# Two graph layers over 32 batches: h of batch 30 and three y tiles of batch 31 in the ring of x, and a new table of planned times

## The chip, the cores and the metric

The kernel runs on one core of a Trainium2 chip. The metric is the time of one launch on the device, in microseconds (us). The engines of the core each run their own queue in order: PE (matrix products), DVE (vector), ACT (scalar functions), POOL (GpSimd), SP (here only an issuer of DMAs). An engine waits at an instruction until what it needs is there, and everything queued behind it waits too.

## The reference

Input x is [32, 512, 1024] (batch, channel c, node n) in f32, adj is [512, 512].

```
h = max(layernorm(x, last axis), 0)
q = sum_c wq[c] h[b,c,n] ;  k = sum_c wk[c] h[b,c,n]
scores[b,m,n] = leaky_relu(k[b,m] + q[b,n], 0.01)
att = softmax(scores over n)
agg[b,c,m] = sum_n h[b,c,n] att[b,m,n]
y = x + relu(adj @ agg + bm)
h = max(layernorm(y), 0)
out = y + einsum('bnf,nm->bmf', h, adj * adj) + bias
```

The last line contracts the channel axis with the elementwise square of adj; bm is added to the last product as well in the kernel's finish step, since turn leaves it out (it adds max(agg, -bm), which is relu(agg + bm) - bm).

## The kernel before

**Layer 0 without the score matrix.** Because a score depends only on the sum of two numbers and leaky relu has two slopes, the softmax of a row splits the nodes, sorted by q, in two sets at one place. So the kernel sorts the nodes by q, forms weighted running sums over the sorted values, and each output node picks two rows out of the running sums. The nodes are 8 blocks of 128, the channels NC = 4 tiles of 128; a sorted table has NB = 9 blocks.

For each batch b these steps run, in this order of data (the name is that of a Python function; the tile that the trace shows stands in brackets):

- load (four x tiles, DMAs on SP, L306), stats0 (DVE, L319), norm0 and slopes0, relu0 in place (ACT, L337);
- scores (PE, pq, then ACT sends it to DRAM), row (ACT's DMA queue reads it back on all partitions, qrow), columns (PE transposes it, pr, to qk);
- rank (DVE, 8 steps, counts how many q are smaller) and to_rows (two halves of 4, gives the scatter rows idx); lower (ACT, 8 steps, counts for the output side) and from_rows (DVE, gives the gather rows idg); factors (DVE and ACT);
- value (PE, pv, 8 steps of 4 products, L454), spread (ACT, PSUM to v, L461), scatter (POOL, 8 indirect DMAs, L467) into a table td in DRAM; there are TABLES = 5 tables;
- fetch (SP, 6 DMAs, L484) reads the sorted table back as vs; weights (ACT, w, L493 and L496), later (DVE, wc and e), totals (PE, pd, L516 and L517, and den on DVE), stationary (POOL, sm, L527, three times for three blocks each);
- scan (PE, sc, 9 steps per batch, L540 and L543), each followed by sums (ACT, L552 to L556: one row each of two vs tiles takes the carry, so that the next scan depends on it; then t, which SP stores to the table);
- gather (POOL, 8 indirect DMAs, L564) into g, of which there is one buffer; excess, divide (DVE), weigh (ACT, L589), combine (DVE, 16 steps, L593);
- reload (four y tiles: x again from HBM, SP, L311), turn (PE transposes g, tr, L600; DVE adds it to y, L602).

Layer 1 is stats1, norm1, slopes1, relu1 (ACT writes h, L337), lift (DVE adds the bias to y, L343), propagate (PE, pg, 8 steps of 4 products, L607), finish (DVE, L615, with the store to out on SP).

**Rings.** x tiles have 7 buffers (pool xp, and 7 more of yp in the first batches), y tiles 7 (yp), h tiles NC = 4 (hp), v 8, vs 5 (three per batch), t 2, g 1. PSUM has 8 banks in one ring. A new tile takes the buffer that was released first and waits for its last reader.

**The order.** Nothing is scheduled automatically. Every step of every batch gets a planned time, b*T + PLAN[name][n] with T = 80.4 (L621), in the first five and last five batches moved by a shift and a stretch from FIRST and LAST (plan, L623). The steps are sorted by this time (L668) and emitted in that order under manual_schedule; each engine's queue is thus a cut of one list. The times serve only to sort. Where batches overlap, PE's list holds value steps of batch b+1, scans of b and b-1, propagate steps of batch b-3 and turns of b-2.

Of the kernel before, what the change touches and what calls it, by code (L numbers as in the profile page):

```python
# [16 lines left out]
P = 128  # L17
# [10 lines left out]
    "adjacency": (-107.86,),  # L28
    "biases": (73.25,),
    "columns": (2.54,),  # L30
    "combine": (
        293.1, 294, 295.37, 296.17, 294.24, 294.54, 295.16, 296.42, 294.48,
        294.66, 293.61, 295.28, 294.87, 296.68, 296.01, 296.52,
    ),
    "compare_mask": (-77.25,),
    "divide": (278.91,),
    "excess": (272.83,),
    "factors": (28.83,),
    "fetch": (74.87,),
    "finish": (357.8, 362.86, 376.29, 376.42, 388.63, 415.81, 401.13, 417.85),  # L40
    "from_rows": (89.36,),
    "gather": (250.12, 258.6, 255.35, 261.49, 268.91, 253.59, 258.29, 256.1),
    "later": (82.34,),
    "lift": (341.79, 343.89, 354.9, 347.45),
    "load": (-125.04, -82.54, -104.22, -58.22),
    "lower": (26.37, 18.82, 14.83, 28.33, 13.66, 12.67, 46.5, 36.18),
    "masks": (-12.78,),
    "norm0": (-27.69,),
    "norm1": (323.91,),
    "pads": (1.15,),  # L50
    "propagate": (347.57, 348.71, 350.13, 365.41, 372.81, 382.23, 382.61, 392.3),
    "rank": (16.85, 14.2, 18.53, 15.82, 17.42, 21.57, 23.3, 23.64),
    "reload": (275.48, 285.03, 274.13, 289.84),
    "relu0": (-17.18, -15.69, -15.67, -14.84),
    "relu1": (334.79, 335.4, 335.54, 338.3),
    "row": (1.98,),
    "scan": (89.28, 94.78, 102.87, 122.08, 139.17, 152.12, 172.91, 183.19, 200.42),
    "scatter": (39.55, 42.53, 43.86, 40.7, 49.58, 45.37, 44.59, 45.6),
    "scores": (-1.83,),
    "slopes0": (-22.22,),  # L60
    "slopes1": (324.32,),
    "spread": (10.78, 16.46, 5.24, 10.37, 28.25, 25.74, 19.08, 20.35),
    "square": (53.38,),
    "stationary": (83.36, 116.24, 162.19),
    "stats0": (-63.29, -60.88, -63.05, -41.14),
    "stats1": (318.79, 319.93, 319.41, 319.38),
    "sums": (89.92, 97.06, 115.14, 127.32, 141.99, 156.22, 174.86, 189.46, 207.26),
    "to_rows": (23, 29.08),
    "totals": (88.21,),
    "turn0": (303.69, 304.68, 304.05, 304.98),  # L70
    "turn1": (312.19, 312.02, 311.8, 312.15),
    "turn_adjacency": (-39.9,),
    "value": (3.89, 14.52, -1.07, 4.1, 20.69, 18.74, 15.77, 15.86),
    "weigh": (286.66, 289.32, 286.94, 289.3, 287.24, 286.87, 287.56, 291.05),
    "weights": (79,),
}
FIRST = {
    "columns": ((-37.98, 0), (-10.89, 0), (-8.73, 0), (-1.59, 0), (-5.53, 0)),
    "combine": ((-1.47, -0.283), (2.11, 0.074), (6.02, -0.446), (-3.46, 1.643), (-3.02, -0.662)),
    "divide": ((0.43, 0), (-4.84, 0), (5.31, 0), (-0.36, 0), (-5, 0)),  # L80
    "excess": ((6.36, 0), (0.71, 0), (9.39, 0), (2.63, 0), (1.02, 0)),
    "factors": ((14.45, 0), (42.49, 0), (37.13, 0), (-13.47, 0), (3.3, 0)),
    "fetch": ((-0.33, 0), (-9.12, 0), (-3.14, 0), (-6.37, 0), (-4.73, 0)),
    "finish": ((0.35, -0.506), (-4.34, -0.255), (-1.3, 0.166), (-13.48, -0.751), (-1, -0.145)),
    "from_rows": ((-17.73, 0), (122.52, 0), (-12.48, 0), (-3.68, 0), (39.28, 0)),
    "gather": ((-3.91, 0.337), (8.03, -0.392), (-0.23, 0.924), (1.48, -0.818), (-10.72, 0.312)),
    "later": ((-6.32, 0), (-2.49, 0), (-5.11, 0), (-3.44, 0), (5.07, 0)),
    "lift": ((5.78, 0.249), (-7.64, -0.77), (14.78, 1.406), (9.87, -0.096), (12.09, 1.113)),
    "load": ((-114.53, -0.719), (-41.9, -0.581), (-61.5, -0.134), (-67.36, 0.974), (-10.03, 0.381)),
    "lower": ((-4.18, -0.847), (-10.86, -0.761), (3.36, -0.598), (31.38, 0.125), (27.64, -0.444)),  # L90
    "norm0": ((-48.85, 0), (-42.24, 0), (-15.97, 0), (-23.37, 0), (-5.52, 0)),
    "norm1": ((-4.55, 0), (0.86, 0), (5.16, 0), (-3.3, 0), (2.66, 0)),
    "propagate": ((3.18, -0.698), (0.66, -0.203), (-2.02, -0.096), (-5.59, -0.325), (1.62, -0.11)),
    "rank": ((-4.4, 0.497), (1.55, -0.098), (-9.21, 1.126), (4.42, 0.365), (7.2, -0.023)),
    "reload": ((2.37, 0.404), (2.84, 0.512), (6.15, -0.047), (4.83, 0.053), (5.08, 0.729)),
    "relu0": ((-52.67, -0.811), (-32.9, 0.887), (-5.05, 1.412), (-5.92, -0.277), (0.27, -0.952)),
    "relu1": ((4.34, 0.844), (-4.2, 0.375), (9.88, -0.496), (1.58, 0.346), (-1.74, -0.782)),
    "row": ((-2.93, 0), (-19.24, 0), (-8.82, 0), (3.92, 0), (-1.39, 0)),
    "scan": ((-8.07, -0.009), (-4.12, 0.027), (-4.42, -0.075), (-2.52, 0.062), (-0.12, -0.002)),
    "scatter": ((19.59, 0.356), (0.39, -0.164), (-11.93, -0.276), (15.6, -0.115), (8.6, 0.613)),  # L100
    "scores": ((-48.13, 0), (-16.76, 0), (-5.07, 0), (-5.89, 0), (-6.97, 0)),
    "slopes0": ((-51.56, 0), (-32.21, 0), (-9.48, 0), (-3.65, 0), (3.28, 0)),
    "slopes1": ((3.12, 0), (1.34, 0), (13.39, 0), (3.58, 0), (5.29, 0)),
    "spread": ((3.65, -0.128), (-4.12, 0.811), (6.73, -0.135), (3.45, 0.185), (7.08, 1.002)),
    "stationary": ((-16.55, -0.278), (-1, 0.017), (-1.03, 0.007), (-4.23, -0.058), (4.88, -0.025)),
    "stats0": ((-86.5, 0.491), (-55.52, 0.533), (-26.5, 0.735), (-39.6, 0.274), (-0.81, 0.405)),
    "stats1": ((-2.32, 0.867), (-1.78, -0.548), (-2.88, 0.916), (-1.4, -0.748), (0.94, 0.179)),
    "sums": ((-4.03, -0.009), (-3.78, 0.04), (-3.01, -0.086), (-3.05, 0.043), (0.68, 0.024)),
    "to_rows": ((-6.46, 0.165), (-1.64, -0.568), (-5.7, -0.361), (5.62, -0.493), (8.82, -0.906)),
    "totals": ((-7.21, 0), (-4.95, 0), (-6.35, 0), (-3.7, 0), (-0, 0)),  # L110
    "turn0": ((1.54, 1.026), (5.01, 1.316), (7.07, -0.842), (11.23, 1.597), (7.25, 0.74)),
    "turn1": ((-5.63, 2.282), (4.23, 0.277), (-3.42, -0.878), (-9.56, -0.462), (0.94, 1.931)),
    "value": ((-14.35, 0.282), (-16.49, 0.638), (-1.63, 0.411), (-4.93, 0.45), (-4.23, 0.018)),
    "weigh": ((-1.72, 0.361), (-2.31, -0.775), (10.15, 0.018), (-5.33, 0.803), (-1.65, 0.186)),
    "weights": ((-3.94, 0), (-0.72, 0), (-2.63, 0), (-0.65, 0), (3.83, 0)),
}
LAST = {
    "columns": ((4.26, 0), (-3.03, 0), (2.37, 0), (-0.77, 0), (3.86, 0)),
    "combine": ((164.15, 0.268), (7.89, -0.595), (-1.54, 0.851), (5.2, 1.047), (1.56, -0.96)),
    "divide": ((162.11, 0), (3.32, 0), (-8.28, 0), (1.71, 0), (-3.58, 0)),  # L120
    "excess": ((127.64, 0), (-3.09, 0), (-3.12, 0), (2.67, 0), (0.92, 0)),
    "factors": ((-11.15, 0), (-18.33, 0), (1.07, 0), (-11.1, 0), (-11.56, 0)),
    "fetch": ((-1.81, 0), (-1.04, 0), (-0.37, 0), (-0.32, 0), (-3.1, 0)),
    "finish": ((699.4, -0.546), (150.27, -0.075), (20.88, 0.53), (4.22, 0.22), (6.11, 0.071)),
    "from_rows": ((13.84, 0), (-28.23, 0), (48.43, 0), (-17.87, 0), (17.41, 0)),
    "gather": ((88.35, 0.017), (-13.92, -0.31), (-9.45, 0.61), (-5.67, 0.718), (-2.02, 0.573)),
    "later": ((7.83, 0), (2.55, 0), (2.21, 0), (-1.95, 0), (-0.28, 0)),
    "lift": ((585.22, -0.837), (120.6, 0.105), (1.56, -0.183), (-6.91, -0.419), (9.05, -0.044)),
    "load": ((1.51, 0.156), (-2.49, 0.009), (4.84, -0.047), (9.16, -0.437), (7.85, -0.154)),
    "lower": ((9.16, 0.14), (-5.44, 0.016), (-5.91, -0.205), (-2.69, 0.118), (-12.14, -0.652)),  # L130
    "norm0": ((-2.04, 0), (-6.51, 0), (-2.65, 0), (-11.04, 0), (5.36, 0)),
    "norm1": ((418.29, 0), (27.36, 0), (-0.04, 0), (-2.45, 0), (1.02, 0)),
    "propagate": ((526.78, -0.74), (151.44, 0.764), (12.38, 0.445), (9.65, 0.206), (11.26, 0.117)),
    "rank": ((4.79, 0.609), (3.43, 0.076), (-8.9, -0.909), (-5.02, -0.932), (1.67, 0.09)),
    "reload": ((184.29, -0.585), (23.97, -0.873), (-3.56, 0.841), (1.54, 0.226), (-3.06, -0.231)),
# [27 lines left out]
def kernel(  # L163
# [169 lines left out]
    def relu(s, layer, c):  # L333
        h = s.x[c]
        if layer == 1:
            h = hp.tile([P, N], F32, tag="h", name=f"h_{s.b}_{c}")
# [362 lines left out]
```

## Time and profile before

| | |
|---|---|
| time before, median of 3 | 2385.05 us (2382.75 to 2387.69) |
| profiled execution | 2390.79 us, span 2389.1 us |
| mean granted clock of PE | 0.985 |
| PE busy | 2298.7 us, 96% of the span |
| DVE, ACT, POOL busy | 1957.4, 1589.4, 719.5 us |
| propagate, L607 | 2048 products, 908.4 us |
| value, L454 | 2048 products, 906.5 us |
| scan, L543 | 1024 products, 287.5 us |
| DMA | 643.45 MB, 269 GB/s over the span |

"Span" is the time between the first and last instruction in the profile. Busy time of PE counts the products; weight loads overlap them. A profile line such as "PE pd L516 <- ACT w L493: 10.2, 3, 4.8" reads: PE stood before line 516 (which writes pd) for ACT's w of line 493, in total 10.2 us, three times, at most 4.8 us. In a table by stretch each line has the window, its length, the busy time of PE, PE's weight loads, DVE, ACT and POOL with the count of their instructions, the granted clock of PE (1.00 is full), the busy share of the DMA engines and GB/s; a table for PE alone has only its busy time.

### The profile page before, as it was taken

The page shows a single profiled execution, that of the slowest core. Times are in us where ns is not written, and L with a number is a line of the kernel's source. Part 1 is how long each engine was busy: PE and PEld are TensorE (multiplying, and loading weights), DVE is VectorE, ACT ScalarE, POOL GpSimd, SP SyncE. Part 2 cuts the span into 40 slices and gives each one's busy share as a digit, 9 for nine tenths or more (in the row PEclk, how much of TensorE's full clock was granted, in tenths as well). Part 3 has the DMA queues.
Part 4 walks back from the last instruction along what each step waited for, and adds up shares of the span by engine and source line. Part 5 has one row for each costly group of instructions (what it writes and reads, how often), then busy time and mean ns, then how long its engine had stood idle before and what let it go on. Part 6 is the DMA issues. An engine that isn't in the chain of part 4 may idle for free.

```text
span 2389.1 us, 28172 instructions
## 1 busy us (share of the span) xinstructions
PE 2298.7 (96%) x7568; PEld 1016.2 (43%) x7568; DVE 1957.4 (82%) x5008; ACT 1589.4 (67%) x2878; POOL 719.5 (30%) x973
## 2 busy tenths in 40 slices
PE   7787999999999999999999999999999999999897
PEld 3233434444444444444444444444444444444343
DVE  6457978788988888988888898888898878889675
ACT  4576666766776766776676677676676856676450
POOL 2233323232332233233223233223323233223310
PEclk9898999999999999999999999999999999999898
DMA  7679887988988998988998888899998888988872
GB/s 231 154 188 279 275 286 256 302 256 269 300 284 284 289 293 258 290 294 268 293 305 261 272 291 285 285 289 282 273 281 277 281 279 250 290 267 282 290 294 87
DMA packets 206895, 643.45 MB, mean 269 GB/s; under 512 B 29120, under 2 KB 29248, under 8 KB 206736
## 3 DMA queue, kind: packets, MB, share of 16 engines
q1 hardware_dynamic: 142944, 355.74, 52.3%
q0 software_dynamic: 57344, 268.99, 30.9%
q10 hardware_dynamic: 6448, 16.92, 2.2%
q8 instruction: 61, 1.00, 0.2%
q14 instruction: 98, 0.80, 0.1%
HBM read 429.94 MB, written 211.60 MB: 269 GB/s over the span
## 4 chain that ended last, share of the span: by engine, by line
PE 84%; DMA 7%; DVE 4%; ACT 3%; issue 1%; SPq 1%; POOL 0%; ACTq 0%; DVEq 0%; POOLq 0%
PE pg L607 35%; PE pv L454 31%; PE sc L543 10%; PE tr L600 4%; DMA vs<-td 3%; PE pq L349 2%; DMA td<-t 2%; PE sc L540 1%; DVE g L593 1%; DVE st L319 1%; DMA qd<-qr 1%; DVE junk L396 1%; DMA wqk<-in_L_gnn_wk_dram 1%; DMA g<-td,idg 1%; SPq L484 0%
## 5 line engine op out<-in xcount | busy, mean ns | idle before, releaser
L607 PE MATMUL pg<-h,wsq 128*128 128x512 f32 x2048 | 908.4, 597 | 12.1 <-ACT h L337 11.9
L454 PE MATMUL pv<-wmT,x 128*128 128x512 f32 x2048 | 906.5, 597 | 1.1 <-ACT x L337 1.0
L607 PEld LDWEIGHTS pg<-h,wsq 128*128 128x128 f32 x2048 | 382.6, 190 | 513.3 <-issue 475.9
L454 PEld LDWEIGHTS pv<-wmT,x 128*128 128x128 f32 x2048 | 381.8, 191 | 495.8 <-issue 457.6
L527 POOL TENSOR_TENSOR sm<-mask_a,wc 128x192 f32<-128x192 f32 x96 | 57.3, 596 | 1128.5 <-DVE wc L504 718.8
L593 DVE SCALAR_TENSOR_TENSOR g<-g,cf 128x512 f32<-128x512 f32 x512 | 363.2, 777 | 6.4 <-ACT g L589 3.6
L467 POOL DMA_INDIRECT td<-v,idx x256 | 285.1, 1114 | 251.7 <-POOL v L466 41.4
L564 POOL DMA_INDIRECT g<-td,idg x256 | 244.0, 953 | 193.9 <-issue 67.9
L543 PE MATMUL sc<-vs,sm 128*64 128x512 f32 x1024 | 287.5, 629 | 12.5 <-ACT vs L552 4.9
L407 ACT ACTIVATE junk<-qrow,qk 128x1024 bf16<-128x1024 f32 x256 | 294.7, 1151 | 6.3 <-DVE qk L370 2.9
L552 ACT COPY vs<-sc 1x512 f32<-1x512 f32 x256 | 145.1, 567 | 214.4 <-PE sc L543 150.3
L602 DVE SCALAR_TENSOR_TENSOR y<-tr,nbm,y 128x512 f32<-128x512 f32 x256 | 176.0, 743 | 56.7 <-PE tr L600 52.0
L615 DVE SCALAR_TENSOR_TENSOR y<-pg,bm_sb,y 128x512 f32<-128x512 f32 x256 | 186.2, 734 | 34.4 <-PE pg L607 34.4
L555 ACT COPY t<-sc 128x512 f32<-128x512 f32 x288 | 168.3, 585 | 66.4 <-DMA td<-t 49.7
L396 DVE TENSOR_SCALAR_CACHE_REDUCE junk<-qrow,qk,cnt 128x896 bf16<-128x896 f32 (+6 forms) x224 | 180.4, 805 | 8.2
L337 ACT ACTIVATE x<-x,nmr,rstd 128x1024 f32<-128x1024 f32 x128 | 148.8, 1231 | 38.4 <-DVE nmr L330 38.4
L391 DVE TENSOR_SCALAR_CACHE_REDUCE junk<-qrow,qk 128x128 bf16<-128x128 f32 (+6 forms) x224 | 164.9, 736 | 8.2 <-issue 2.4
L461 ACT COPY v<-pv 128x512 f32<-128x512 f32 x256 | 140.6, 583 | 44.8 <-issue 28.3
L319 DVE BATCH_NORM_STATS2 st<-x 128x6 f32<-128x512 f32 x256 | 162.1, 675 | 7.1 <-DMA x<-in_x_dram 7.1
L589 ACT ACTIVATE g<-g,cf 128x512 f32<-128x512 f32 x256 | 163.4, 712 | 1.9 <-DVE cf L583 1.9
L343 DVE TENSOR_TENSOR y<-y,bias_sb 128x1024 f32<-128x1024 f32 x128 | 156.6, 1230 | 7.9 <-ACT h L337 7.9
L319 DVE BATCH_NORM_STATS2 st<-y 128x6 f32<-128x512 f32 x256 | 159.1, 663 | 0.0
(111 smaller groups left out, 1913.3 us busy)
## 6 DMA issues: line engine op xcount, KB each, us to landing
vs<-td SPq DMA_DIRECT2D x192, 384.8 KB
td<-t SPq DMA_DIRECT2D x576, 128.2 KB
x<-in_x_dram SPq DMA_DIRECT2D x128, 512.0 KB
y<-in_x_dram SPq DMA_DIRECT2D x128, 512.0 KB
out_dram<-y SPq DMA_DIRECT2D x128, 512.0 KB
qrow<-qd ACTq DMA_DIRECT2D x32, 512.0 KB
td<-v,idx POOLq DMA_INDIRECT x256, 8.3
g<-td,idg POOLq DMA_INDIRECT x256, 13.4
```

The lines of the kernel that those rows point to most:

```text
L319: nc.vector.bn_stats(st[:, i, :], s.x[c][:, ts(i, HALF)])
L396: nc.vector.tensor_scalar(junk[:, j * P :], s.qrow[:, j * P :], qc, first, ALU.is_lt, ALU.add, accum_out=s.cnt[:, 1, j : j + 1],)
L407: nc.scalar.activation(junk, s.qrow, AF.Sign, bias=s.qk[:, 1, j : j + 1], accum_out=s.sgn[:, j : j + 1])
L454: nc.tensor.matmul(pv, s.h[c][:, ts(j, P)], wmT[:, c, :], start=(c == 0), stop=(c == NC - 1))
L467: i = nc.gpsimd.indirect_dma_start(tds[s.b % TABLES][:, :], bass.IndirectOffsetOnAxis(ap=s.idx[j // 4][:, j % 4 : j % 4 + 1], axis=0), v[: ...
L543: nc.tensor.matmul(p[ts(k, HP), :], m[:, k, :], s.vs[h][:, 0:C], start=True, stop=True)
L555: nc.scalar.copy(t[:, 0:C], p)
L564: nc.gpsimd.indirect_dma_start(s.g[:, j, :], None, tds[s.b % TABLES][0 : 3 * NB * HP, :].rearrange("(s k) w -> s (k w)", k=3), bass.Indire ...
L593: nc.vector.scalar_tensor_tensor(r, s.g[:, j, k * W : k * W + C], s.cf[:, k, j : j + 1], r, ALU.mult, ALU.add)
L602: nc.vector.scalar_tensor_tensor(xh, pt, nbm[:, o : o + 1], xh, ALU.max, ALU.add)
L607: nc.tensor.matmul(pg, wsq[:, r, ts(c, P)], s.h[r][:, ts(i, HALF)], start=(r == 0), stop=(r == NC - 1),)
L615: nc.vector.scalar_tensor_tensor(xh, s.pg.pop((c, i)), bm_sb[:, c : c + 1], xh, ALU.add, ALU.add)
```

## The change

Four things, none of which adds or drops a product, a vector step or a DMA:

- h tiles of batch 30 (B - 2) are taken from the ring of x instead of that of h;
- y tiles 0, 1 and 2 of batch 31 are taken from the ring of x instead of that of y;
- load and reload have a planned time and shifts for each of the four tiles;
- all times in PLAN, FIRST and LAST, and T, are new.

The last one changes the order of the queues. On PE the steady batches keep their order except for a few exchanges: value step 3 before 0, propagate (3, 0) before (2, 1), one turn step later, scan 2 of batch b before scan 7 of batch b - 1. The first five and last five batches change more. On ACT the order needs two more loads of function tables (123 for 121), among the first and the last batches.

```diff
 PLAN = {
...
-    "load": (-125.04, -82.54, -104.22, -58.22),
+    "load0": (-132.547,),
+    "load1": (-83.561,),
+    "load2": (-110.642,),
+    "load3": (-58.45,),
...
-    "propagate": (347.57, 348.71, 350.13, 365.41, 372.81, 382.23, 382.61, 392.3),
+    "propagate": (346.423, 349.207, 352.169, 365.765, 371.233, 382.761, 381.981, 389.706),
-    "rank": (16.85, 14.2, 18.53, 15.82, 17.42, 21.57, 23.3, 23.64),
+    "rank": (17.984, 18.872, 20.129, 19.992, 25.594, 25.16, 26.367, 26.318),
...
-    "scan": (89.28, 94.78, 102.87, 122.08, 139.17, 152.12, 172.91, 183.19, 200.42),
+    "scan": (88.672, 94.082, 102.974, 119.344, 135.342, 151.67, 171.394, 183.726, 197.836),
...
-    "to_rows": (23, 29.08),
+    "to_rows": (21.507, 28.041),
...
-    "value": (3.89, 14.52, -1.07, 4.1, 20.69, 18.74, 15.77, 15.86),
+    "value": (4.654, 14.383, -2.141, 4.319, 19.868, 19.769, 15.801, 17.456),
...
     def reload(s, c):
-        t = yp.tile([P, N], F32, tag="y", name=f"y_{s.b}_{c}")
+        pool, tag = (xp, "x") if s.b == B - 1 and c < NC - 1 else (yp, "y")
+        t = pool.tile([P, N], F32, tag=tag, name=f"y_{s.b}_{c}")
...
         if layer == 1:
-            h = hp.tile([P, N], F32, tag="h", name=f"h_{s.b}_{c}")
+            pool, tag = (xp, "x") if s.b == B - 2 else (hp, "h")
+            h = pool.tile([P, N], F32, tag=tag, name=f"h_{s.b}_{c}")
...
-    T = 80.4
+    T = 80.647
...
         for f in (
-            load, reload, lift, rank, lower, value, spread, scatter, to_rows, scan, sums, gather,
-            weigh,
+            lift, rank, lower, value, spread, scatter, to_rows, scan, sums, gather, weigh,
         ):
...
+        for c in range(NC):
+            plan(s, load, f"load{c}", c, args=((),))
+            plan(s, reload, f"reload{c}", c, args=((),))
```

FIRST and LAST hold a pair (shift, stretch) for each of five batches and each name in the same way, all of them new.

## The prediction

> **What bounds the kernel now.** I read the page first, then a table of engine time by stretch of the span, then the waits of PE, then the chain that ended last.
>
> ```profile
> span 2389.1 us, 28172 instructions
> PE 2298.7 (96%) x7568; PEld 1016.2 (43%) x7568; DVE 1957.4 (82%) x5008; ACT 1589.4 (67%) x2878; POOL 719.5 (30%) x973
> ```
>
> PE is busy for 2298.7 of 2389.1 us, so a new order of the same work can win at most the 90 us in which it stands, plus what a slow clock costs. The table by stretch (PE's time first, then the other engines, the granted clock, DMA) says where those lie:
>
> ```profile
> 60.00:160.00 100.00, 82.25 (x245) 31.17 (x248) 51.17 (x176) 69.55 (x135) 24.60 (x44) 0.91 0.63 157
> 160.00:200.00 40.00, 36.12 (x110) 13.58 (x102) 26.57 (x92) 18.36 (x45) 11.92 (x16) 0.96 0.95 292
> 200.00:250.00 50.00, 36.89 (x144) 18.02 (x145) 38.84 (x99) 37.21 (x69) 18.99 (x25) 0.86 0.93 281
> ...
> 300.00:600.00 300.00, 293.26 (x974) 130.24 (x972) 245.15 (x638) 205.21 (x372) 91.78 (x123) 0.99 0.85 273
> 600.00:1200.00 600.00, 599.77 (x1980) 265.25 (x1977) 522.88 (x1349) 424.86 (x770) 194.85 (x261) 1.00 0.90 286
> ...
> 2200.00:2250.00 50.00, 40.03 (x128) 18.39 (x128) 31.38 (x68) 26.31 (x53) 11.53 (x14) 0.86 0.94 292
> ...
> 2340.00:2390.00 50.00, 33.65 (x93) 15.91 (x90) 22.07 (x35) 4.93 (x5) 0.00 (x0) 0.83 0.16 63
> ```
>
> From 600 to 1200 us PE is full, and the next 600 us are alike (600.00 of 600): no order gains there, it can only lose. PE stands for 34.7 us between 60 and 250 (the first batches fill the pipeline), 6.7 in 300 to 600, 10.0 in 2200 to 2250, 16.3 in the last 50; the first 14.3 are the load of wqk, which stays. What PE waits for, up to 300 us and then from 2150 on:
>
> ```profile
> PE sc L540 <- ACT vs L553: 11.7, 3, 7.7
> PE pd L516 <- ACT w L493: 10.2, 3, 4.8
> PE tr L600 <- DVE g L593: 4.4, 1, 4.4
> ...
> PE pg L607 <- ACT h L337: 11.9, 2, 10.7
> PE pd L516 <- ACT w L493: 7.5, 1, 7.5
> PE sc L543 <- ACT vs L552: 2.3, 1, 2.3
> ```
>
> "pd waits for w" is the arrival of a batch's fetch from the table, ACT's weights being a 0.5 us step behind it. The chain shows the loop of the fill: fetch lands, DVE ranks the next batch, indices, eight scatters on POOL, next fetch. The last fetch of the fill, and a hand-over of the tail (start, us, what):
>
> ```profile
> 222.04 10.77 DMA vs<-td
> ...
> 2292.69 7.14 DMA y<-in_x_dram
> 2299.83 2.63 DVE y L602 x4
> ```
>
> In the fill pd of batches 0 to 4 starts at 70.6, 119.5, 169.7, 235.2 and 308.6, each 0.4 to 2.4 us after its fetch has landed (70.2, 119.0, 169.3, 232.8, 308.2). So a stall between two of these gains nothing by going away, unless the next fetch lands earlier: PE would only wait longer at the next pd. The prices of what is moved: a propagate or value step is 3.5 us, a scan about 1.0, a turn step 0.44.
>
> **The change part by part.**
>
> *The two ring edits.* h of batch 30 no longer waits for the readers of h of batch 29, h of batch 31 no longer for those of batch 30; three y tiles of batch 31 no longer wait for an out transfer. In the trace h_31 is computed at 2352.44, when its slopes are just ready (2351.97), 12.9 us after batch 30's last propagate ended; h_30 at 2309.72 with slopes at 2309.63 and pg_29 ended at 2309.79. The y_31 reloads land by 2336.0, its turn starts at 2340.3. So what hides these waits is the chain turn, stats, slopes; with it gone they'd cost at most the 1.2 us by which pg_30 starts late. By themselves: 0 to 1.2 us, I take 0.
>
> *The order in the fill.* On SP the 20 stores of padding now go at about 14 us, ahead of the loads of x_2, whose value steps start at 101; on POOL the square of wsq moves behind the first scatters, read first by propagate at 260: both 0, with 20 us and more of cover. Batch 1's first four scatters now follow four ranks on DVE rather than six, so their indices come 4 us earlier. The second four need all eight ranks: a stats step (1.5 us) no longer stands between, they come 1.4 us earlier, and these set the fetch (issued at 105.28, when the last scatter had landed at 105.13). Against this, relu of batch 1 moves behind the last spread of batch 0 and pq_1 behind a value step, so ACT issues qrow_1 about 5 us after its present 59.77; that took 10.2 us beside fetch 0 and landed at 69.97, and the rank starts at 71.9. Both transfers share the engines, so I expect 70 to 73. Fetch 1: 0 to 2 us earlier, I take 1. Fetch 2 is behind the sums of scan 1_4 on SP: 0.7 earlier. Fetch 3: POOL's scatters begin at 197 only because stationary 2_3 ahead of them waits for scan 2_2 (ends at 195.9), indices being there at 194.5; PE now does scan 2_2 before two value steps. Excess of batch 0 is put ahead of the indices on DVE (0.6 us; its gather landed by 193.0). Net: fetch 3 1.8 earlier. Also scan 2_6 (1.0 us) now stands before pd_3, in its wait. PE is 2.8 us ahead at pd_3. The 7.7 and 4.4 us stalls (scan 2_4, turn 0) shrink, since sums 2_3 go ahead of weigh on ACT and combine 0 ahead of from_rows 1, but this is the time that pd_3 then waits: counted zero.
>
> Fetch 4 was issued at 289.2, 3.4 us after its scatters had landed, since SP had to pass the sums of scan 3_4 and an out store that waited for finish behind combine on DVE. Scan 3_4 now comes two propagate steps earlier, the finish comes before combine, and three lifts, factors and excess (6.7 us) leave the path of batch 4's indices, two stats (2.9) join it. The fetch then is issued some 6 us earlier; a reload of y that needs a freed buffer now stands directly before it. Then pd_4's 2.8 us wait and the 2.2 for e inside it go, and so does the slow clock behind them (scans 4_0, 3_6, 4_1 took 5.9 us for 3): together 5, leaving half of the clock. Fill: 2.8 + 5 = 7.8 us.
>
> *The steady part.* Per batch: two value steps and two propagate steps swap, one turn step comes after a propagate, scan 7 and scan 2 swap; on SP a reload and an out store change places before the fetch. PE is full, the fetch of these batches lands ahead of pd, and ACT's two added table loads (2 x 1.28 us, among the first and last batches) lie in an engine that is 67% busy: 0. If cover failed, half a microsecond in each of 22 batches would cost 11. The 1.1 us wait at 526 and the 5.4 in batches 26 to 28 change places; I take 1 gained.
>
> *The tail.* Fetch 31 stays behind the sums of scan 30_4 on SP, so pd_31 stays late. Two propagate steps of batch 27 go before the last value steps of batch 31, which end 7 us later on PE; the scatter lands at 2203.1 and SP is free at 2205.9, so most of it is covered, since ACT's spread ran late anyway. Scan 30_6 moves into the wait (1.0). Then propagate steps of batch 28 stand between the scans of batch 31, where PE had waited 2.25 us:
>
> ```profile
> 2227.00:2231.00 4.00, 3.81 (x16) 0.50 1.02 424
> 2231.00:2235.00 4.00, 1.75 (x5) 0.50 1.01 416
> ```
>
> Row: after the wait the clock stays at 0.50 until about 2236, so pd and five scans (5.3 us at full clock) took from 2226.8 to 2238.6, 2.25 of it waiting: 4.3 lost to the clock. The nearest dense restart is pg_31: its first step took 6.55 instead of 3.6, 2.95 lost. The Trainium skill (TensorE: Matmul & The Clock Gate, "The HAM clock gate") says that about 3.4 us of sustained work restores the clock, so 1.7 would be lost. By the row the denser order gains 2.25 + 4.3 - 2.95 = 3.6, by the rule 4.9. But relu of batch 28 now follows the sums of 30_6 on ACT (1.8 us) and propagate must wait for it: I take 3, with the scan in the wait. Combine 29, gather 30 and combine 30 follow at the same pace, since finish 28 comes earlier with PE. The y_30 reloads go ahead of the sums of 31_8 on SP; they landed at 2299.8 and held the last turns, so up to 1.2 us at pg_30: I take 0.7. The 10.7 us before pg_31 stay: turn 31 still follows all of pg_30. Tail: 3.7.
>
> *Sum.* 7.8 + 1 + 3.7 = 12.5 us. The profiled execution took 2390.79 us (span 2389.1), so it would be 2378; it stands 5.7 above the median of three, 2385.05, which becomes 2372.5.
>
> **The rivals.** A measurement of this kernel tells about 0.2% (4.8 us) from no change.
>
> *Nothing of the fill arrives.* Fetch 3 and 4 land as before (qrow_1 eats the ranks' gain, the reload ahead of fetch 4 waits for its buffer); only the scan in pd_3's wait and the tail count: 4 to 5 us, 2380.5. For it: five landings set the fill. Against: fetch 4's delay on SP is visible. Chance 0.18.
>
> *All of it.* Fetch 4 comes early enough that the waits and slow clock to 600 us vanish (6.7), and those of batches 26 to 28 (5.4): 20 us, 2365, down to 2358. Chance 0.14.
>
> *Tail eaten by the g chain.* One g buffer: combine 30 ended at 2295.87 and turn 30 started at 2295.83. If combine 29 does not come earlier, PE waits there and the tail gives 0.7: 2375.5. Inside the forecast.
>
> *Slower.* The steady order puts a turn step after a propagate and a value step before another: should one of DVE's in-order steps then wait (turn of y after the others, with finish and the next ranks queued behind it), the indices and the fetch come later in every batch. Fetch 7 was late by 1.1 us, so the margin is small there. From 0.6 us in each of 22 batches on it eats the 12.5; at 0.9 it gives 2392. Against: five batches of fill at their worst cost PE waits, yet 600 to 1800 has none, so slack grew. Chance 0.06.
>
> *The rings do nothing.* By the trace they do not; this is in the forecast.
>
> **How the numbers follow.** Forecast (9 to 17 us gained, 2368 to 2376): 0.62, likeliest 2372.5. With the no-fill rival on the upper side and the full gain on the lower, 2361 to 2383 leaves out 2 in 10. Faster by over 0.2% (below 2380.3): the forecast, the full gain and half of the no-fill rival, 0.85. Within 0.2%: 0.09. Slower: 0.06.
>
> **What would show it.** Right: pd_3 near 232, pd_4 near 301 with no wait, a clock of 1.00 from 250 on; PE waits for w below 3 us after 230; in the tail pd_31's wait about 6.5 and no vs wait behind it; h wait still near 10.7. Wrong: pd_4 later than 306, PE below 599 in 600 to 1200, or turn 30 waiting for g by over 2 us.

## The result and the profile after

| | before | changed |
|---|---|---|
| median, 8 runs each on one chip | 2388.49 us (2382.75 to 2395.61) | 2373.48 us (2370.14 to 2378.16) |
| profiled execution, its span | 2390.79, 2389.1 us | 2374.61, 2372.9 us |
| mean granted clock of PE | 0.985 | 0.987 |

The ratio is 0.9938, 95% interval [0.992, 0.9956]: 15.0 us faster. The prediction said 2372.5 us, which was 12.5 us below the first three runs of before (median 2385.05); the median of eight lies 3.4 us higher.

The head of the page of the changed kernel:

```profile
span 2372.9 us, 28069 instructions
PE 2295.2 (97%) x7568; PEld 1011.5 (43%) x7568; DVE 1952.6 (82%) x5008; ACT 1599.8 (67%) x2880; POOL 720.7 (30%) x973
```

The work is the same (7568 recorded products, ACT with the two added table loads), so the 16.2 us of the span are standing time of PE and slow clock. The table by stretch (PE's busy time after the length of the stretch, granted clock and DMA share near the end) shows where:

```profile
60.00:160.00 100.00, 81.60 (x228) 31.10 (x226) 49.55 (x176) 68.78 (x134) 24.82 (x44) 0.91 0.66 163
200.00:250.00 50.00, 35.97 (x138) 17.28 (x139) 35.61 (x91) 32.31 (x63) 21.61 (x27) 0.83 0.83 248
300.00:600.00 300.00, 299.92 (x997) 132.36 (x996) 260.17 (x673) 208.26 (x380) 96.87 (x130) 1.00 0.90 283
600.00:1200.00 600.00, 600.00 (x1980) 264.93 (x1979) 516.55 (x1336) 431.30 (x776) 197.31 (x260) 1.00 0.92 284
1800.00:2100.00 300.00, 299.32 (x988) 131.96 (x987) 257.94 (x654) 217.21 (x392) 89.69 (x123) 1.00 0.89 285
2200.00:2250.00 50.00, 47.59 (x147) 20.42 (x146) 39.31 (x82) 27.58 (x54) 14.31 (x19) 0.97 0.96 313
```

From 300 to 600 PE stood for 6.7 us and now stands for 0.1. The fill itself is no better: PE stands for 18.4 us from 60 to 160 (17.8 before) and 14.0 from 200 to 250 (13.1). From 1800 to 2100, a stretch that the prediction did not show, the row of before is

```profile
1800.00:2100.00 300.00, 294.00 (x966) 129.61 (x963) 252.79 (x648) 207.15 (x376) 96.82 (x125) 0.99 0.90 278
```

so 5.3 us of standing time went there. PE's waits in the changed kernel: the larger ones up to 300 us (without the 13.5 us before the first product), then all from 300 to 2130, then the larger ones from 2150:

```profile
PE sc L636 <- ACT vs L649: 11.8, 3, 8.9
PE sc L639 <- POOL sm L623: 11.1, 3, 4.4
PE sc L639 <- ACT vs L648: 8.1, 5, 3.0
...
PE tr L696 <- DVE g L689: 0.7, 1, 0.7
PE sc L639 <- ACT vs L648: 0.7, 1, 0.7
...
PE pg L703 <- ACT h L433: 12.8, 3, 10.3
PE pd L612 <- ACT w L589: 2.1, 1, 2.1
PE sc L639 <- ACT vs L648: 0.8, 1, 0.8
```

From 300 to 2130 PE now waits 1.4 us in all. But in the fill scans wait for POOL's stationary operand, 11.1 us, where pd had waited 10.2 for w. In the new order scan 0 stands ahead of pd in batches 0, 1, 3 and 4 (in the old order only in batch 3). Its operand comes from wc, and wc from w, so it is the same fetch that is waited for under another name. The line of the chain that holds pd_3 is

```profile
224.42 11.12 DMA vs<-td
```

which lands at 235.54; the one of before landed at 232.81.

**An account by batch.** The start of pd of a batch is a good mark, since it waits for the fetch. Where scan 0 of a batch stands ahead of its pd, the mark is the start of that scan, so the mark of batch 3 lies 0.9 us (before) and 1.6 us (changed) ahead of pd itself. Each row is a difference of two such marks in microseconds. The first two columns are the two profiled executions; the next two are means over profiles of this study whose order in that stretch is the old one or the new one (with the extremes and their number), the experiments below among them.

| stretch | before | changed | old order | new order | gained |
|---|---|---|---|---|---|
| start to pd_3 | 234.2 | 237.0 | 232.0 (227.9 to 235.4), 6 | 233.3 (230.7 to 237.0), 5 | -1.4 |
| pd_3 to pd_4 | 74.4 | 72.1 | 74.6 (73.9 to 76.1), 4 | 72.0 (71.2 to 73.4), 5 | 2.6 |
| pd_4 to pd_5 | 74.6 | 71.1 | 74.7 (74.5 to 75.2), 4 | 72.0 (70.8 to 73.0), 8 | 2.7 |
| pd_5 to pd_8 | 215.1 | 212.1 | 216.1 (215.1 to 218.1), 6 | 212.4 (211.9 to 215.7), 8 | 3.7 |
| pd_8 to pd_25 | 1200.1 | 1198.9 | 1200.0 (1199.3 to 1200.4), 5 | 1199.0 (1198.9 to 1199.0), 7 | 1.0 |
| pd_25 to pd_29 | 292.0 | 282.9 | 291.6 (289.6 to 294.0), 5 | 283.5 (282.8 to 285.9), 8 | 8.0 |
| pd_29 to pd_31 | 136.4 | 137.9 | 137.3 (130.8 to 146.0), 5 | 137.3 (134.7 to 141.6), 7 | 0.0 |
| pd_31 to the last product | 157.5 | 156.1 | 156.8 (156.0 to 157.5), 5 | 156.1 (154.9 to 157.8), 5 | 0.6 |

The start of the kernel differs by up to 7 us between profiles, in either order, so the 1.4 us lost there are not clear of that spread. The stretches from pd_3 to pd_8 and from pd_25 to pd_29 repeat, and they carry the gain: 9.0 and 8.0 us. The rows add up to 17.2 us, the medians differ by 15.0.

### The profile page after: what moved, and what is told of

Its sections match the earlier page's. It is cut to its first block, busy times and chain, and to the rows that moved or that the text cites. A ratio compares the mean times of both kernels' runs of the same rounds, so it can differ in the third digit from the quotient of the medians.

```text
span 2372.9 us, 28069 instructions
## 1 busy us (share of the span) xinstructions
PE 2295.2 (97%) x7568; PEld 1011.5 (43%) x7568; DVE 1952.6 (82%) x5008; ACT 1599.8 (67%) x2880; POOL 720.7 (30%) x973
## 4 chain that ended last, share of the span: by engine, by line
PE 85%; DMA 5%; DVE 5%; ACT 2%; issue 1%; POOL 1%; SPq 0%; ACTq 0%; another core or an unknown queue 0%; POOLq 0%; DVEq 0%
PE pg L703 34%; PE pv L550 33%; PE sc L639 10%; PE tr L696 4%; DMA vs<-td 2%; PE pq L445 2%; PE sc L636 1%; DVE g L689 1%; DVE st L414 1%; DMA g<-td,idg 1%; DMA td<-v,idx 1%; DVE junk L492 1%; ACT x L433 0%; DVE junk L487 0%; DMA x<-in_x_dram 0%
## 5 line engine op out<-in xcount | busy, mean ns | idle before, releaser
L623 POOL TENSOR_TENSOR sm<-mask_a,wc 128x192 f32<-128x192 f32 x96 | 51.9, 540 | 1254.9 <-DVE wc L600 785.7
L689 DVE SCALAR_TENSOR_TENSOR g<-g,cf 128x512 f32<-128x512 f32 x512 | 357.9, 756 | 46.4 <-ACT g L685 44.3
L563 POOL DMA_INDIRECT td<-v,idx x256 | 272.4, 1064 | 149.3 <-POOL v L562 36.3
L639 PE MATMUL sc<-vs,sm 128*64 128x512 f32 x1024 | 282.6, 621 | 21.3 <-POOL sm L623 11.1
L503 ACT ACTIVATE junk<-qrow,qk 128x1024 bf16<-128x1024 f32 x256 | 294.0, 1148 | 5.5 <-DMA qrow<-qd 2.5
```

The source lines that it names most:

```text
L503: nc.scalar.activation(junk, s.qrow, AF.Sign, bias=s.qk[:, 1, j : j + 1], accum_out=s.sgn[:, j : j + 1])
L563: i = nc.gpsimd.indirect_dma_start(tds[s.b % TABLES][:, :], bass.IndirectOffsetOnAxis(ap=s.idx[j // 4][:, j % 4 : j % 4 + 1], axis=0), v[: ...
L639: nc.tensor.matmul(p[ts(k, HP), :], m[:, k, :], s.vs[h][:, 0:C], start=True, stop=True)
L689: nc.vector.scalar_tensor_tensor(r, s.g[:, j, k * W : k * W + C], s.cf[:, k, j : j + 1], r, ALU.mult, ALU.add)
```

## Experiments

**1. Halves and parts.** Two kernels join the orders at batch 16: in the first, batches 0 to 15 have the new times and 16 to 31 the old (with old rings); in the second it is the other way round (with new rings). Two more separate the rings from the order. The second kernel has `b < 16` in the line shown; the tables, T and t0 are those of the order that `old(s.b)` names.

```diff
+def old(b):
+    return b >= 16
...
-            t = s.b * T + t + shift + stretch * (t - mean)
+            t = t0 + t + shift + stretch * (t - mean)
```

> Batches 0 to 15 in the new order, 16 to 31 in the old one, old rings. Theory (read from the two traces, by the start of pd of a batch): the first half has won 6.9 us by batch 16, nearly all of it between batches 4 and 8 and nothing before batch 4, so this kernel is 7 us faster than before (ratio 0.997), and pd of batch 3 and 4 still start later than before. Rival (what the prediction said): the fill itself gave some 8 us, most of it before batch 4; then pd of batch 4 starts some 6 us earlier than before here. Second rival: the 0.8 us by which the profiled runs differ by chance in each stage adds up, and the head is worth under 3 us.

Measured: 2377.57 us, ratio 0.9952 [0.9936, 0.9968] to before on the same chip: 11.7 us by the medians, more than the theory's 7. By the account the new head gives 7.6 us up to pd_8. pd_3 and pd_4 were not late here (232.0 and 304.1), as the first theory had said, but that is the start, which varies.

> Batches 0 to 15 in the old order, 16 to 31 in the new one, new rings. Theory: the second half has won 9.3 us, 9 of them between pd of batch 26 and pd of batch 29, where the waits of the trace before (5.4 us, with a slow clock behind them) are gone, and next to nothing after pd of batch 31: 9 us faster than before (ratio 0.996). Rival (the prediction): the last batches' tail after pd of batch 31 gives 4 and batches 26 to 29 give 1, so 5 us in all. If the two halves are independent, this and the first half add up to the 15 us of the whole change.

Measured: 2393.17 us, 1.0017 [1.0005, 1.0029]. This kernel pays for its own joint. From pd_8 to pd_16 it took 575.7 us where before takes 565.1, and two of the waits of PE from 300 to 2000 are new

```profile
PE pg L842 <- ACT t L790: 4.2, 1, 4.2
...
PE tr L835 <- ACT t L790: 1.3, 1, 1.3
```

They stand at 1080 and 1159 us, where batches of the two orders meet on ACT. From pd_16 to its last product it took 1211.6 us against 1221.0 in before. So its total says nothing of the tail, while its stretch pd_25 to pd_29 (283.3 us) does.

For the rings alone, before with only the two ring edits, and the changed kernel without them:

```diff
-        t = yp.tile([P, N], F32, tag="y", name=f"y_{s.b}_{c}")
+        pool, tag = (xp, "x") if s.b == B - 1 and c < NC - 1 else (yp, "y")
+        t = pool.tile([P, N], F32, tag=tag, name=f"y_{s.b}_{c}")
...
-            h = hp.tile([P, N], F32, tag="h", name=f"h_{s.b}_{c}")
+            pool, tag = (xp, "x") if s.b == B - 2 else (hp, "h")
+            h = pool.tile([P, N], F32, tag=tag, name=f"h_{s.b}_{c}")
```

> The kernel before, in its own order on every queue, with only the two ring edits. Theory: the waits that they remove are covered by turn, stats and slopes, so 0 us (0 to 1.2 gained); the wait of pg for h stays at 10.7 and 1.2. Rival: the edits free the stores and reloads of the last batch and give 2 us or more.

> The changed kernel in its own order on every queue, without the two ring edits. Theory: as fast as the changed kernel, 15 us faster than before (ratio 0.994). Rival: the new order needs the rings, because it puts h of batch 30 and the reloads of y of batch 31 earlier than buffers come free; then 2 to 5 us of the gain are lost and a wait of pg for h or of DVE for y appears in the last 100 us.

Measured: 2387.27 us, 0.9995 [0.998, 1.001] with the rings alone; 2374.75 us, 0.9926 [0.9899, 0.9954] with the order alone. Within these intervals all of the gain is the order's. PE's largest wait after pd_31 with the rings alone:

```profile
PE pg L609 <- ACT h L339: 11.5, 2, 10.3
```

h is late because its slopes are, and a free buffer for it changes nothing.

**2. What made pd_4 to pd_5 slow.** In before POOL issues two gathers of g_2 at 293.56 and 294.87, right behind the pieces of fetch 4, which takes 19.0 us from its first issue to its last landing (289.21 to 308.20). In the changed kernel all eight stand behind the stationary operand of batch 4 (from 307.79), and the fetch takes 14.6 us (287.44 to 302.04). POOL of before, then of the changed kernel, by start and duration:

```profile
293.56 1.00 POOL L564 DMA_INDIRECT g<-td,idg  x1 [10.20 <-PE tr L600]
294.87 0.95 POOL L564 DMA_INDIRECT g<-td,idg  x1 [0.30 <-issue]
311.01 0.51 POOL L527 TENSOR_TENSOR sm<-mask_a,wc 128x192 f32<-128x192 f32 x1 [15.19 <-DVE wc L504]
```

```profile
306.66 0.51 POOL L623 TENSOR_TENSOR sm<-mask_a,wc 128x192 f32<-128x192 f32 x1 [26.02 <-DVE wc L600]
...
307.79 1.00 POOL L660 DMA_INDIRECT g<-td,idg  x1 [0.15 <-issue]
```

First, before with only these two gathers moved (put_after(x, y) takes step x out of the sorted list and puts it behind y):

```diff
     steps.sort(key=lambda e: e[:2])
+    put_after((gather, 2, 5), (stationary, 4, 0))
+    put_after((gather, 2, 0), (stationary, 4, 0))
```

> The kernel before with one exchange on POOL: the first two gathers of batch 2, which stood ahead of stationary of batch 4, stand behind it (where the changed order has them). Every other queue is as before. Theory: these two gathers start beside the fetch of batch 4 and stretch its last pieces from 6.6 to 15 us; without them the fetch lands near 300 instead of 308, the waits at pd of batch 4 (2.8 and 2.2 us and the slow clock after them) go, pd of batch 5 starts 5 us earlier, and the kernel is 5 us faster than before (ratio 0.998). Rival: what the changed order won there came from scan 3_4 and the finish steps that were moved; then nothing changes here, or the later gather makes the combine of batch 2 late and costs 1 to 3 us.

Measured: 2375.02 us against 2375.94 for before on this chip, 0.9992 [0.9984, 1.0]. Fetch 4 took 15.1 us (284.14 to 299.20) and pd_4 waited 0.8 us for w, but pd_4 to pd_5 stayed at 75.7 us. So the fetch came early, as the theory said, and the 5 us did not come. PE's waits in this kernel from 295 to 500:

```profile
PE pd L517 <- DVE e L508: 2.3, 1, 2.3
PE pd L516 <- ACT w L493: 0.8, 1, 0.8
```

So e was late of itself. DVE and ACT of before show why:

```profile
310.41 0.18 DVE L328 RECIPROCAL rstd<-std 128x4 f32<-128x4 f32 x1 [8.26 <-ACT std L324]
...
310.70 0.36 DVE L504 TENSOR_SCALAR wc<-w,ident 128x9 f32<-128x9 f32 x2
310.97 0.19 DVE L508 TENSOR_TENSOR_SCAN e<-runs,w 128x20 f32<-128x20 f32 x1
```

```profile
308.28 0.30 ACT L493 ACTIVATE w<-vs,nq 128x3 f32<-128x3 f32 x1 [1.69 <-DMA vs<-td]
...
308.79 1.28 ACT L324 ACT_TABLE_LOAD   x1
310.08 0.30 ACT L324 ACTIVATE std<-mv,eps_sb 128x4 f32<-128x4 f32 x1
```

DVE stood 8.26 us at slopes of batch 1. These need std, which ACT's queue holds behind the weights of batch 4, and then a table load of 1.28 us comes between. Behind the slopes on DVE stand wc and e, which pd_4 needs. PE waits for an engine that waits for another's queue, and the line of PE's waits names only the last link. The test is the kernel above with one more line:

```diff
+    put_after((slopes, 1, 1), (totals, 4))
```

> The kernel before with the two gathers of g_2 behind the stationary operand of batch 4 on GpSimd, and the slopes of batch 1 behind e of batch 4 on VectorE. Theory (pd_4 waited for e because VectorE stood at those slopes, which waited for ScalarE): the stretch pd_4 to pd_5 falls from 75 to about 72 us, and the time is 0.998 of the kernel before. Rival (e was late for another reason): the stretch stays at 75 us and the ratio at 0.999 to 1.000.

Measured: 2390.65 us, ratio 0.9976 [0.9959, 0.9993] to before on a third chip. pd_4 to pd_5 fell to 72.5 us, that of the new order (72.0). PE from 300 to 500 waits for e only 0.3 us:

```profile
PE pd L517 <- DVE e L508: 0.3, 1, 0.3
```

The theory holds. pd_5 to pd_8 stayed at 216.0, as in the old order, so those 3.7 us are another stall: the one before pd_7 (1.1 us in before). The traces say what PE waits for there: in all six profiles of the old order pd_7 starts 0.4 us after fetch 7 has landed, in the eight of the new order 1.3 to 2.0 us after it. The fetch takes as long in both (13.5 to 15.2 us), but is issued 58.0 to 60.0 us after pd_6 in the old order and 55.0 in the new. Which moved step brings that issue forward no edit here singled out. Slow clock is no part of it in before: its row shows 1.00 from 515 to 600 us.

**3. pd_25 to pd_29.** In before the shifts of LAST reach to batches 27 and 28 and put their indices (to_rows) and scatters late, but not their ranks: the last rank of batch 27 starts 47 us ahead of pd_27, the first scatter at 1905.98, 38 us ahead (43 and 45.5 us in batch 25). In the changed kernel that scatter starts at 1886.80, 47 us ahead. PE's larger waits in before from 1869 to 2091:

```profile
PE pd L516 <- ACT w L493: 2.1, 1, 2.1
PE sc L543 <- DVE den L521: 1.6, 1, 1.6
PE sc L543 <- POOL sm L527: 0.9, 1, 0.9
PE sc L543 <- ACT vs L552: 0.8, 1, 0.8
```

Before with the shifts of LAST for the last three batches only:

```diff
-        elif B - 1 - s.b < len(LAST.get(name, ())):
+        elif B - 1 - s.b < min(3, len(LAST.get(name, ()))):
```

> The kernel before without the shifts of the last table for batches 27 and 28, which so run at the times of a steady batch; batches 29 to 31 keep theirs. Theory: the 8 us that the change wins between pd of batch 26 and pd of batch 29 come from no longer delaying the ranks, scatters and fetches of batches 27 and 28; here they are on time too, pd 25 to pd 29 takes 283 us instead of 292, and the kernel is 8 us faster, less whatever batches 29 to 31 lose by meeting steady neighbours (up to 4). Rival: the shifts are needed because the two following batches have theirs; then the stretch stays at 290 or more.

Measured: 2385.29 us, 1.0043 [1.003, 1.0056]. The stretch fell to 282.3 us (289.6 in the kernel of part 2 on the same chip), PE waiting for nothing in it, and the scatters of batch 27 started 46 us ahead of pd_27. So the shifts of these two batches are the cause. But the run takes all of them away at once, and late scatters are not what pd_27 waited for: fetch 27 of before had landed at 1941.0, 3.3 us ahead of it. The shifts also put row of batch 28 ahead of the weights of batch 27 in ACT's queue, and ACT stood 8.0 us there until q and k of batch 28 were in DRAM (7.9 to 8.1 us in all five profiles with the old tail). ACT of before:

```profile
1939.92 0.58 ACT L552 COPY vs<-sc 1x512 f32<-1x512 f32 x1 [8.01 <-DMA qd<-qr]
...
1943.17 0.30 ACT L493 ACTIVATE w<-vs,nq 128x3 f32<-128x3 f32 x1
```

With only the last three batches shifted the whole is slower all the same, for the last batch is late. PE's waits from 2078 to 2250:

```profile
PE pd L516 <- ACT w L493: 12.0, 1, 12.0
PE sc L543 <- ACT vs L552: 2.9, 2, 2.4
PE pd L517 <- DVE e L508: 2.2, 1, 2.2
```

The last two pieces of fetch 31 were held up on SP until a scan had freed their vs buffer:

```profile
SPq L484 <- PE sc L543: 8.8, 1, 8.8
```

So the shifts of batches 27 and 28 were the price, in the old order, of an early batch 31. The changed order has the one without the other: its pd_31 waits 2.1 us.

**4. Why pd_3 did not come earlier.** In the changed kernel DVE has excess of batch 0 ahead of the scatter indices of batch 3, and excess needs the last gather of g_0. That landed at 196.29 (at 192.96 in before). DVE, changed kernel:

```profile
196.41 0.17 DVE L669 TENSOR_TENSOR cf<-g,arg 128x8 f32<-128x8 f32 x1 [3.47 <-DMA g<-td,idg]
```

The same wait was 3.5, 1.7, 1.5 and 1.3 us in four more profiles of this order. Excess and divide put behind the indices:

```diff
+    put_after((excess, 0), (to_rows, 3, 1))
+    put_after((divide, 0), (excess, 0))
```

> The changed kernel with excess and divide of batch 0 on DVE behind both halves of to_rows of batch 3 (as in the order before). Theory: DVE stood 1.3 to 3.5 us at excess for the gather of batch 0, with the indices of batch 3 queued behind it, and this is why fetch 3 came no earlier; here fetch 3 is issued 1.5 to 4 us earlier, pd of batch 3 and 4 start 1.5 to 4 us earlier, and the kernel is 2 us faster than the changed one (ratio 0.993 to before). Rival: the end of the scatters is set by POOL's pace and the transfers beside it; then pd of batch 3 stays at 231 to 237.

Measured: 2366.8 us, 0.9962 [0.995, 0.9975] on the chip of part 2, where the changed kernel was not run, so that the time cannot be set against it. The wait was gone:

```profile
192.36 0.17 DVE L669 TENSOR_TENSOR cf<-g,arg 128x8 f32<-128x8 f32 x1 [0.19 <-issue]
```

Fetch 3 is issued 46.3 us after pd_2 (45.4 to 47.3, three profiles with this edit), against 49.5 (49.0 to 50.8, five of the changed order) and 48.8 (47.5 to 51.3, six of the old). pd_2 to pd_3 is 63.7 us with the edit (62.8 to 64.7), 65.9 in the changed order (64.5 to 67.5), 64.6 in the old (63.3 to 66.5). So excess cost 3.2 us at the issue and 2.2 at pd_3, as the theory said.

**5. The wait that stayed at the end.** PE waits 10.3 us before pg_31, since turn 31 stands behind all of pg_30 on PE. One propagate step of batch 30 put behind turn 31, with four finishes of batch 30 behind the slopes of batch 31 on DVE:

```diff
+    for c, i in ((2, 0), (3, 0), (2, 1), (3, 1)):
+        put_after((finish, 30, c, i), (slopes, 31, 1))
+    put_after((propagate, 30, 3, 1), (turn, 31, 0, 3))
```

> The changed kernel with the turns of batch 31 one propagate step earlier on PE (before the last of batch 30) and on DVE the last four finish steps of batch 30 behind slopes of batch 31. Theory: combine of batch 31 ends 2.2 us before the turns start, so the chain turn, stats, slopes, h of the last batch starts 2.3 to 3 us earlier, the wait before its first propagate falls from 10.3 to about 4.5 (the propagate step moved into it takes 3.5) and the kernel ends 2.3 us earlier (ratio 0.993). Rival: the turns then wait for combine, or the four finishes delay lift and the stores, and nothing is won.

Measured: 2367.31 us, 0.9961 [0.9948, 0.9975], on that same chip, so this time too cannot be set against the changed kernel. PE from 2280 to 2345:

```profile
PE pg L703 <- ACT h L433: 8.4, 2, 6.6
PE tr L696 <- DVE g L689: 1.3, 1, 1.3
```

The wait fell by 3.7 us to 6.6, not to 4.5, for turn 31 (at 2317.02) now waits 1.3 us for the combine of batch 31, as the rival said. From the first product of pg_30 to the end: 70.1 us in three profiles with this edit, 73.2 in five of the new order without it.

**6. The edits together, beside the changed kernel.**

> The changed kernel unaltered, as the measure for the two runs beside it on the same chip. Every theory: 0.992 to 0.996 of the kernel before.

Measured: 2376.2 us, 0.9926 [0.99, 0.9952].

> The changed kernel with both single edits: excess of batch 0 behind the row transposes on VectorE, and turn 31 ahead of the last down projection of batch 30. Theory (the two waits lie in different places, so the gains add): 3 to 4 us from fetch 3 and 2.3 us from the wait for h_31, together 5 to 6 us below the changed kernel beside it. Rival (what the head gains is lost again at the landing of fetch 31, which the ring sets): 2 to 3 us below it.

Measured: 2371.77 us, 0.9905 [0.9878, 0.9931] to before; against the changed kernel beside it, by the means of six runs each, 4.2 us faster (interval 0.7 to 7.6), ratio 0.9983 [0.9968, 0.9997]. It beats both kernels. The interval holds the theory's 5 to 6 and the rival's 2 to 3, so it does not decide between them.

A third edit: PE's transposes of batch 31 (pr_31) wait 1.2 to 3.1 us for ACT's qr_31 (the copy of pq_31 that goes to DRAM), which stands behind the weights of batch 30. They were put one value step later:

```diff
+    put_after((columns, 31), (value, 31, 3))
```

> The kernel of the run before with the column transposes of batch 31 (pr_31) one value step later on TensorE, since pr_31 waited 2.0 to 2.8 us for ScalarE's qr_31, which stands behind weights w_30. Theory: the wait goes and the stretch pd_29 to pd_30 falls by 2.5 us, the time by about 2 us below the run before. Rival: the gain is taken back by a longer wait at pd_31 for fetch 31, and the time is the same within 0.5 us.

Measured: 2372.3 us, 0.9909 [0.9883, 0.9934]: no gain. From the run before to this one, a profile each, pd_29 to pd_30 fell by 3.3 us (74.9 to 71.6), and pd_30 to pd_31 rose by 2.7 (62.8 to 65.4). That is the rival, with a correction: the wait at pd_31 itself is 1.5 us in both, and others ahead of it took what was won, as PE's waits from 2070 to 2215 show for this kernel (the waits for vs were at most 0.8 us in the run before):

```profile
PE tr L696 <- DVE g L689: 2.1, 2, 1.4
PE sc L639 <- ACT vs L648: 2.0, 2, 1.5
PE pd L612 <- ACT w L589: 1.5, 1, 1.5
```

From pd_29 to the landing of fetch 31 it took 136.7 us, and 137.3 in the run before. In all fourteen profiles of this study pd_31 starts 0.4 us after fetch 31 has landed: the landing sets this stretch, and a wait of PE ahead of it cost next to nothing.

## Why the prediction was right, and where it was not

The total was right (2372.5 against 2373.5), and by luck: of the four terms that were not zero one held, the errors of the other three cancel, and the gain, 15.0 us where 12.5 were predicted, started from a median 3.4 us above that of the first three runs. In each case the measured size is from the means of the account.

- **pd_3, 2.8 us predicted: nothing won** (1.4 lost by the means, within their spread). The step that failed is "Excess of batch 0 is put ahead of the indices on DVE (0.6 us; its gather landed by 193.0)". It took the landing of the gather from the old order, and in the new one it was 196.3 in the profile after: excess then holds up the indices by 1.3 to 3.5 us, and the first scatter of batch 3 starts at 199.0, where it was 197.5. Part 4 shows the mechanism: counted from pd_2, fetch 3 was to be issued 1.8 us earlier, was issued 0.8 later, and without this one step 2.4 earlier. So the other moves counted there did help. (One reading was off besides: scan 2_2 now stands ahead of three value steps, not two.) The sign that was named, pd_3 near 232, did not come: pd itself starts at 238.6, and started at 235.2. "pd_4 later than 306" did (309.1 by the mark), though without a wait; the start alone moves pd_4 by 7 us in either order, so it was a poor sign.
- **pd_4 and the e behind it, 5 us predicted: 5.3** (2.6 and 2.7). The size held, and the waits went as said. Of the cause a part was missing. Counted from pd_3, fetch 4 was to be issued some 6 us earlier and was issued 5.4 us earlier (50.15 against 55.54, means of five and six profiles; by the clock of the two profiles 1.8, since pd_3 was late). Another 4 us come from the gathers that ran beside it (part 2: 19.0 us with them, 15.1 without). And e came in time because DVE no longer stood at the slopes. The prediction had not looked at what POOL and DVE held behind and ahead of that fetch.
- **The middle, 1 us predicted: about 13** (3.7 to pd_8, 1.0 to pd_25, 8.0 to pd_29). This term was the most mis-sized. "The 1.1 us wait at 526 and the 5.4 in batches 26 to 28 change places" assumed that they would come back elsewhere; they did not. The rival "all of it" was right on this point. With the 5.4 us of waits go smaller stops and slow clock (0.91 from 1930 to 1950 in before), for 8 in all. That PE is full in the steady part held: 600.00 of 600, and the rival "slower" found no wait to feed on.
- **The tail, 3.7 us predicted: 0.6.** What was argued for the scans of batch 31 came. The wait for vs behind pd_31 was gone (the 0.8 us that are left stand at 2255.6), the clock from 2200 to 2250 rose from 0.86 to 0.97, and pg_29 starts 46.2 us after pd_31 where it took 49.3 (means of five profiles each): 3.1 us. By pg_30 1.3 us of them are left. The step that failed is "Combine 29, gather 30 and combine 30 follow at the same pace", and with it "up to 1.2 us at pg_30: I take 0.7": instead of a further gain, 1.8 us were lost between pg_29 and pg_30. Of PE's waits there, those of 0.8 us for vs and 0.7 for h_29 are small, and the one for h_30 grew from 1.2 to 1.8 us. More than that the waits do not say; the chain of the changed kernel has four finish steps among DVE's turns and stats of batch 30, that of before has two. So the rival "tail eaten by the g chain" had the size (0.7), but its wait did not come: turn 30 waits for g by 0.2 us at most. Between pd_29 and pd_31 nothing was won, since fetch 31 lands no earlier after pd_29. The wait at pd_31 was said to be 6.5 and was 2.1, but as pd_31 is set by a landing, that is no gain by itself (part 6).
- **The rings, 0: held** (part 1). **h_31's wait near 10.7: 10.3, held.**

What the slow clock behind pd_31 costs can be read from two rows of the changed kernel (pd_31 starts at 2212.1):

```profile
2212.00:2216.00 4.00, 3.66 (x16) 1.56 (x16) 2.30 (x8) 3.95 (x7) 1.95 (x3) 0.68 1.02 423
2216.00:2220.00 4.00, 4.00 (x10) 1.44 (x8) 1.83 (x3) 3.95 (x6) 0.00 (x0) 0.89 1.01 411
```

They lost 4 x 0.32 and 4 x 0.11, 1.7 us. That agrees with the rule that the prediction cites from the Trainium skill (TensorE: Matmul & The Clock Gate, "The HAM clock gate"), about 3.4 us of work at half clock, and not with the 2.95 us that it took from the row of pg_31.

Open: which of the moved steps brings fetch 7 earlier, what holds up batch 30 between pg_29 and pg_30, which of the shifts of batches 27 and 28 cost what, and where the 1.0 us from pd_8 to pd_25 comes from, with PE waiting 0.3 us at most in either kernel.

## What to carry to other kernels

A list of steps sorted by planned times loses time where a step of one batch that still waits stands in a queue ahead of a step that another batch needs: read DVE's, ACT's and POOL's waits ahead of each late landing, for a wait of PE names only the last link. A step moved ahead of a critical one must be costed with the landing it will see in the new order, not in the old. And find which landing sets a stretch before paying to remove a wait upstream of it: 3.3 us won ahead of fetch 31 gave nothing back.

## What the hardware showed

Gathers beside a fetch stretch its last pieces. Fetch 4 in the old order took 18.5 to 19.4 us with two of them (four profiles), and 15.1 us in each of the two kernels of part 2 that moved them away. For fetch 31 there is no such exchange, only what came together. In the old order its last piece took 12.2 us where all six pieces were issued ahead of the first gather of g_29; 13.6 and 16.6 where one came after it, 19.3 where two, 23.8 where four did (five profiles). Only in the kernel of part 3, whose last two pieces were issued 9 us behind the others, did it take 11.0 with two after the gather. In the last kernel of part 2, that with 23.8 us, PE stood before pd_31 for

```profile
PE pd L516 <- ACT w L493: 16.5, 1, 16.5
```

against 7.5 in before (16.6 us), 11.2 with 19.3 us and 1.9 with 12.2. In seven of the eight profiles with the new order of the last batches and no gather ahead, it took 11.3 to 13.4 us, in the eighth 16.9. In the old order this hangs on a microsecond or two between SP and POOL.

On three chips the kernel before took 2375.9, 2389.3 and 2396.9 us (medians of 19, 53 and 19 runs), and the changed kernel took 2376.2 on the third: the three differ by more than this change is worth. That the meeting at fetch 31 is a part of it is a guess that no run tested.
